# Gate and up products summed in one PSUM bank, with the next outer product's first two products moved between: a decoder layer on one core

## The chip, the cores and the metric

The kernel runs on one core of one Trainium2 chip. The metric is the device time of one execution in microseconds (us). A core has five engines with a queue each: TensorE (PE in the profile, with its weight loads as PEld), VectorE (DVE), ScalarE (ACT), GpSimd (POOL) and SyncE (SP). The program puts matmul results in PSUM banks of 128 x 512 float32, and the other engines copy or add them from there. In this trace an engine's instructions start in the order of its queue, and one that waits holds up those behind it, a DMA's issue included.

## The reference

`x` is [16, 128, 1024] in float32. The reference is one decoder layer:

```python
x = x + attn(layernorm(x))              # one head of 4 of width 1024: 256 wide
x = x + xattn(layernorm(x), ctx_4096)   # linear attention, 8 heads of 64, output normalised
x = x + ffn(layernorm(x))

# ffn:
Wg, Wu, Wd = dequantize(...), dequantize(...), dequantize(...)   # int4, groups of 64
g = jnp.einsum('bsh,ih->bsi', x, Wg)      # h = 1024, i = 2752
u = jnp.einsum('bsh,ih->bsi', x, Wu)
h = jax.nn.silu(g) * u
return jnp.einsum('bsi,hi->bsh', h, Wd)
```

The change touches the products g and u and what turns them into h.

## The kernel before

**Stages.** Self-attention lasts to about 250 us, the second attention to about 806, with its tail beside the first products of the FFN until about 870. The gate and up products follow until 1893, and the down projection until the end. Tokens are in two passes of eight batches; a pass's 1024 tokens are two halves of TB = 512. The 2752 rows of gate and up are eleven blocks: ten of 256 (two halves of 128), and a remainder, RB, of 192. NI = 5 pairs of blocks make the ten.

**Seven products for eight.** All FFN products use the Strassen-Winograd scheme: a 2 x 2 block product takes seven products of sums of blocks. The operands are T1 to T7 on the token side (T1, T2, T3 are blocks themselves; 5, 6, 7 and 4 are differences) and seven weight tiles. The four results are (0,0) = P1+P2, (1,1) = P1+P6+P5+P7, (1,0) = P1+P6+P7+P4 and (0,1) = P1+P6+P5+P3. Some sums are made by accumulating products in one PSUM bank, the rest by DVE.

**Pass 0** (812 to 1388 us, `one_block` and `products`, matmul on line 1069): for each of eleven blocks, a set of seven products of gate and one of up. Each product is eight matmuls (one per K chunk) of 512 columns. The order is `GATE` = 1, 5, 6, 7, 2, 3, 4. A set takes four banks: P1 with P2, P5 with P3, P6 alone, P7 with P4. ScalarE copies P1 (line 1078); DVE adds P6 into `u` (L1081) and P5 into `v` (L1082), then P7 + v, P2's bank as it stands, P3 + u and P4 + u give the results. Gate results go through Silu on ScalarE, up results are multiplied by them into `h`, which is stored to DRAM by `put_stores` (L1019) from ScalarE's queue.

Beside pass 0, the weights of later blocks and of the down projection are made ready by `prepare` (lines 185 to 245): raw int4 is loaded, taken apart and scaled by DVE (`pa`, lines 215 to 217), combined into the seven tiles (`pc`, line 231), and stored to DRAM from ScalarE's queue. One step is taken after those products with `n % 7 in (0, 2, 4, 5)`, and after each product of block 0 once the attention is over (`beside`). Near the end of pass 0, `outer_operand` (L1048) makes pass 1's T5, T6, T7 and T4 on DVE.

**Pass 1, two levels** (1388 to 1845, `two_levels`): for the ten whole blocks the seven outer products of a pair of blocks (order `DOWN` = 1, 2, 6, 5, 3, 7, 4) are each split again into seven inner products of eight matmuls of 256 columns. 35 outer products (5 pairs i by 7 q) of seven inner products (order `INNER2` = 6, 1, 5, 7, 2, 3, 4) run one after the other. GpSimd makes an outer product's left operands (`li`) from weight tiles, DVE the right ones (`ti`; kept from i = 0 for q = 1, 6, 3, 4). ScalarE copies inner P6 (`iu`), DVE adds P1 to it, then P5 for `iv`, and then sums the results into U, V and C over the outer products. After q = 2, 3, 7 and 4 a quadrant C is finished: Silu on ScalarE, `h` on DVE. For the down projection's own seven products `combine_h` makes sums `hc` of h of this pass and h of pass 0, loaded back as `hl`; of each pair of blocks DVE makes one block's and GpSimd the other's. `hc` too are stored by `put_stores` from ScalarE's queue.

**Order.** Instructions through `InOrder` (line 52) stay in the order of the program: in `two_levels` that is TensorE, DVE and GpSimd. Elsewhere the tile scheduler may move instructions of an engine. Small DVE operations of `two_levels` that are not a product's drain wait in a queue `extra`, of which `do_extra` takes one or two after each product. Weight tiles come by SP's queue, in pairs, `AHEAD` = 4 pairs before they are used. The remainder block of pass 1 follows (1845 to 1893), and then the down projection (L1541).

Of the kernel before, what the change touches and what calls it, by code (L numbers as in the profile page):

```python
# [11 lines left out]
F32 = mybir.dt.float32  # L12
# [26 lines left out]
GATE = (1, 5, 6, 7, 2, 3, 4)  # L39
# [16 lines left out]
def decoder_layer(  # L56
# [45 lines left out]
    xt3 = ctx.enter_context(tc.tile_pool(name="xt3", bufs=2, side="right", reuse_waits="tile"))  # L102
# [486 lines left out]
    if True:  # L589
# [156 lines left out]
        def turned(b):  # L746

            xns = []
            for n in range(2):
                xn = xt3.tile([P, C // 2], F32, name="xn3")  # L750

                rows = X[b].rearrange("p (g j e n) -> p n j g e", g=16, j=JC, n=2)[:, n]
                dst = xn.rearrange("p (j g e) -> p j g e", j=JC, g=16)
                normalise_act(dst, rows, b)
                xns.append(xn)
            nc.gpsimd.dma_start(x_all[b], X[b])
            later(2, lambda: turn_rows(b, xns, btr, b2))
            if b == B - 1:
                blocks.update(new_blocks(xlate, lambda k: f"X{HB + 2 * k}"))
                loads = block_loads(0, blocks)  # L760
                for n in range(8):
                    later(7 + 2 * n, lambda: next(loads))
# [170 lines left out]
    with ExitStack() as gs:  # L933
# [29 lines left out]
        HALF = [("g", 1), ("g", 2), ("u", 1), ("u", 2)]  # L963

        def sequence(ps, blk):
            todo = [(mat, q) for mat in "gu" for q in GATE]
            if ps == blk == 0:

                todo = HALF + [k for k in todo if k not in HALF]
            return todo  # L970

        def tiles_of(ps, blk):
            todo = [(blk, *k) for k in sequence(ps, blk)]
# [4 lines left out]
            [t for blk in range(len(BLOCKS)) for t in tiles_of(0, blk)]  # L978
            + [[(2 * i + f, mat, q) for mat in "gu"] for i, q in OUTERS for f in range(2)]
            + tiles_of(1, RB)  # L980
# [34 lines left out]
        def put_stores(now=False):  # L1015
            for st in stores:
                st[0] -= 1
            while stores and (now or stores[0][0] < 0):
                nc.scalar.dma_start(*stores.popleft()[1:])  # L1019
# [29 lines left out]

        def products(blk, mat, T, got):  # L1050
# [4 lines left out]
            def temp(name):  # L1055
                bufs = 2 if name == "p1" else 1
                t = kept[name] = ct.tile([P, TB], F32, name=name, tag=name, bufs=bufs)[:w]
                return t

            def product(q):  # L1060
                wt = next_weights(w)
                put_stores()
                first = {2: 1, 3: 5, 4: 7}.get(q, q)
# [4 lines left out]
                for j in range(JC):  # L1068
# [5 lines left out]
                        stop=(q in (2, 6, 3, 4) and j == JC - 1),  # L1074
                        skip_group_check=True,
                    )
                if q == 1:
                    nc.scalar.copy(temp("p1"), ps)
                elif q == 6:
                    u2 = temp("u2")  # L1080
                    nc.vector.tensor_tensor(u2, ps, kept["p1"], ALU.add)  # L1081
                    nc.vector.tensor_tensor(temp("v"), bank[5], u2, ALU.add)  # L1082
                elif q == 7:
                    got((1, 1), ps, kept["v"])
                elif q == 2:
                    got((0, 0), ps, None)
                elif q == 3:
                    got((0, 1), ps, kept["u2"])
                elif q == 4:
                    got((1, 0), ps, kept["u2"])  # L1090
# [3 lines left out]
        def one_block(ps, blk, T, between):  # L1094
# [38 lines left out]
            for n, (mat, q) in enumerate(sequence(ps, blk)):  # L1133
# [10 lines left out]
        INNER2 = (6, 1, 5, 7, 2, 3, 4)  # L1144
        KEPT = {1: "X8", 6: "X10", 3: "X12", 4: "X14"}
# [4 lines left out]
        def inner_right(T, q, vector=nc.vector):  # L1150
# [9 lines left out]
            def comb(k):  # L1160
                if k == 5:
                    pool, tag = (xlate, KEPT[q]) if q in KEPT else (deep_pool[0], "ti")
# [12 lines left out]
        def inner_left(L):  # L1175
# [9 lines left out]
            def comb(k):  # L1185
                t = L[k] = ct.tile([P, 2, CHUNKS, P], F32, name="li", tag="sg")
                a, b, op = {
                    5: (A(1, 0), A(1, 1), ALU.add),
                    6: (L.get(5), A(0, 0), ALU.subtract),
                    7: (A(0, 0), A(1, 0), ALU.subtract),  # L1190
# [4 lines left out]
            return {k: lambda k=k: comb(k) for k in (5, 6, 7, 3)}  # L1195
# [4 lines left out]
        def two_levels(T, ready):  # L1200
            tensor, vector, gpsimd = (
                InOrder(tc, e) for e in (nc.tensor, nc.vector, nc.gpsimd)
# [7 lines left out]
            extra = deque()  # L1210

            def do_extra(n=None):
                for _ in range(len(extra) if n is None else min(n, len(extra))):
                    extra.popleft()()

            L = ready
            U = V = C = None
            hs = {}
            for n, (i, q) in enumerate(OUTERS):
                banks.rotate(1)  # L1220
                if q == DOWN[0]:
                    U = deep_pool[0].tile(wide, F32, name="U")
                elif q == 5:
                    V = deep_pool[0].tile(wide, F32, name="V")
                load_weights()
                following = {}
                left = inner_left(following) if n + 1 < len(OUTERS) else {}
                if n + 1 < len(OUTERS):

                    extra.extend(inner_right(T, OUTERS[n + 1][1], vector))  # L1230
                if q == 3:
                    halves = {1: load_first(i, 1)}
                bank = {}
                u = v = None

                def got(ib, src, add):
                    k = 2 * ib[0] + ib[1]
                    add_to = vector.tensor_tensor
                    if q == 1:
                        if add is None:  # L1240
                            nc.scalar.copy(U[:, k], src)
                        else:
                            add_to(U[:, k], src, add, ALU.add)
                        return
                    dst, base = {2: (C, U), 6: (U, U), 5: (V, U), 3: (C, V), 7: (C, V), 4: (C, U)}[q]
                    if add is None:
                        if q == 7:
                            add_to(U[:, k], src, U[:, k], ALU.add)
                        add_to(dst[:, k], src, base[:, k], ALU.add)
                        return  # L1250
                    m = V if q == 5 else C
                    add_to(m[:, k], src, add, ALU.add)
                    if q == 7:
                        add_to(U[:, k], U[:, k], m[:, k], ALU.add)
                    add_to(dst[:, k], m[:, k], base[:, k], ALU.add)

                for p in INNER2:
                    set_ = {2: 1, 3: 5, 4: 7}.get(p, p)
                    if set_ == p:
                        bank[p] = banks[0].tile([P, 2, HT], F32, name=f"q{p}", tag="gu")  # L1260
                    ps = bank[set_]
                    for m in range(2):
                        for c in range(CHUNKS):
                            tensor.matmul(
                                ps[:, m, :],
                                L[p][:, m, c, :],
                                R[q, p][:, c, :],

                                start=(set_ == p and m == c == 0),
                                stop=(p in (6, 2, 3, 4) and c == CHUNKS - 1),  # L1270
                                skip_group_check=True,
                            )
                    put_stores()
                    if p == 6:
                        u = ct.tile([P, 2, HT], F32, name="iu", tag="p1", bufs=2)
                        nc.scalar.copy(u, ps)
                    elif p == 1:
                        vector.tensor_tensor(u, ps, u, ALU.add)
                    elif p == 5:
                        v = ct.tile([P, 2, HT], F32, name="iv", tag="v", bufs=1)  # L1280
                        vector.tensor_tensor(v, bank[5], u, ALU.add)
                        for k in (5, 6):
                            if k in left:
                                left[k]()
                    elif p == 7:
                        if q not in (1, 5):

                            C = deep_pool[0].tile(wide, F32, name="C")
                        got((1, 1), ps, v)
                        if left:  # L1290
                            left[7]()
                    elif p == 2:
                        got((0, 0), ps, None)
                    elif p == 3:
                        got((0, 1), ps, u)
                        if left:
                            left[3]()
                    elif p == 4:
                        got((1, 0), ps, u)
                    do_extra({6: 0, 1: 1, 7: 1}.get(p, 2))  # L1300
                load_weights()
                if q in (2, 3, 7, 4):
                    s, half = {2: (0, 0), 3: (0, 1), 7: (1, 1), 4: (1, 0)}[q]
                    nc.scalar.activation(C[:, :, 0], C[:, :, 0], AF.Silu)
                    finish = []
# [348 lines left out]
```

## Time and profile before

| | us |
|---|---|
| runs of before | 2366.76, 2368.12, 2372.04; median 2368.12 |
| profiled execution | 2371.64 |
| its span | 2369.9 |
| TensorE busy in it | 2304.6 |

By stage, from the same profiled execution (busy us of an engine in the stretch):

| stretch, us | stage | PE | DVE | ACT | POOL |
|---|---|---|---|---|---|
| 0-250 | self-attention | 239.4 | 167.6 | 36.7 | 56.5 |
| 250-812 | second attention | 549.0 | 471.1 | 326.4 | 138.7 |
| 812-1388 | pass 0 of gate and up | 563.0 | 349.0 | 69.1 | 9.0 |
| 1388-1845 | pass 1, two levels | 433.0 | 377.2 | 42.0 | 247.1 |
| 1845-1893 | pass 1, remainder block | 48.0 | 18.5 | 4.5 | 5.8 |
| 1893-2370 | down projection | 472.2 | 242.2 | 8.1 | 0.0 |

The profiled execution is one, and its times are read against its own 2371.64. Names in the profile are the program's tiles: `q` is a PSUM bank of an inner product, `p` one of pass 0's, `w` a weight tile, `wg<-pa` a store of prepared gate weights. L52 stands for all that goes through `InOrder`, so there the tile names tell what an instruction is. "[2.54 <-DVE iu L52]" behind an instruction says that its engine was idle for 2.54 us before it and that the DVE operation writing `iu` ended the wait.

### The profile page before, as it was taken

How to read it: one execution, taken by the hardware profiler on the slowest of the kernel's cores; microseconds unless marked ns; L12 is line 12 of the kernel's file. 1: busy time of each engine (PE TensorE's matmuls, PEld its weight loads, DVE VectorE, ACT ScalarE, POOL GpSimd, SP SyncE). 2: the span in 40 equal slices, each digit the busy share in tenths (PEclk: the TensorE clock that was granted, in tenths of full speed). 3: DMA queues.
4: the chain of work that ended last, by engine and by line, in shares of the span. 5: the costliest groups of instructions: out<-in, count | busy, mean ns of one | idle time of the engine just before them, and what ended most of it. 6: DMA issues, size and time to landing. Idle time of an engine off the chain costs nothing.

```text
span 2369.9 us, 25410 instructions
## 1 busy us (share of the span) xinstructions
PE 2304.6 (97%) x8976; PEld 1589.8 (67%) x8976; DVE 1625.4 (69%) x2318; ACT 486.8 (21%) x771; POOL 457.0 (19%) x321
## 2 busy tenths in 40 slices
PE   8999999999999899999899999999999999999999
PEld 7556566666666554444344468778778488888888
DVE  6694788888879639997641179788887474444562
ACT  2111356566656440000000000000010000000000
POOL 4120122222222200000000035564564100000000
PEclk9999999999999999999999999999999999999999
DMA  6232366566685549999953224553553864544631
GB/s 237 74 121 86 121 168 185 179 178 183 191 242 170 169 141 344 357 365 351 305 185 102 74 93 131 172 186 107 178 203 101 295 214 144 166 143 144 214 111 36
DMA packets 275774, 424.69 MB, mean 179 GB/s; under 512 B 26752, under 2 KB 124928, under 8 KB 275520
## 3 DMA queue, kind: packets, MB, share of 16 engines
q1 hardware_dynamic: 207824, 310.52, 42.5%
q10 hardware_dynamic: 65520, 104.16, 12.2%
q0 software_dynamic: 2304, 8.39, 0.9%
q8 instruction: 72, 1.18, 0.2%
q14 instruction: 54, 0.44, 0.1%
HBM read 265.62 MB, written 157.35 MB: 178 GB/s over the span
## 4 chain that ended last, share of the span: by engine, by line
PE 76%; DVE 13%; DMA 7%; issue 2%; ACT 1%; SPq 0%; POOL 0%; ACTq 0%; DVEq 0%; POOLq 0%
PE po L1541 20%; PE p L1069 14%; PE q L52 12%; PE mm L52 11%; PE kq L52 8%; PE mm L368 5%; PE tr L52 3%; DVE hc L52 2%; PE mm L383 2%; DVE C L52 2%; PE mm L264 2%; DVE pa L216 1%; DVE pa L217 1%; DVE pc L231 1%; DMA wg<-pa 1%
## 5 line engine op out<-in xcount | busy, mean ns | idle before, releaser
L1069 PE MATMUL p<-b,w 128*128 128x512 f32 (+1 forms) x768 | 344.2, 599 | 16.2 <-DVE v L1082 6.2
L1069 PEld LDWEIGHTS p<-b,w 128*128 128x128 f32 (+1 forms) x768 | 143.1, 188 | 204.1 <-issue 185.8
L1069 PE MATMUL p<-T,w 128*128 128x512 f32 (+1 forms) x576 | 255.1, 592 | 0.0
L52 POOL TENSOR_TENSOR li<-w 128x512 f32<-128x512 f32 x70 | 97.5, 1393 | 564.1 <-DVE h L1113 501.7
L1069 PEld LDWEIGHTS p<-T,w 128*128 128x128 f32 (+1 forms) x576 | 106.8, 185 | 140.0 <-issue 136.2
L52 PE MATMUL q<-ti,li 128*128 128x256 f32 x840 | 192.8, 379 | 0.6 <-DVE ti L52 0.6
L1541 PE MATMUL po<-wc,lc 128*128 128x256 f32 x840 | 183.4, 379 | 0.0
L52 PEld LDWEIGHTS q<-ti,li 128*128 128x128 f32 x840 | 159.5, 190 | 23.1 <-POOL li L52 1.0
L1541 PEld LDWEIGHTS po<-wc,lc 128*128 128x128 f32 x840 | 159.6, 190 | 21.8
L684 POOL TENSOR_TENSOR qe<-qe,qden 128x1024 f32<-128x1024 f32 x64 | 121.7, 1901 | 266.1 <-DVE qden L52 231.7
L1541 PE MATMUL po<-wq,lq 128*128 128x256 f32 x560 | 126.7, 379 | 0.4 <-issue 0.4
L52 PE MATMUL mm<-kh,cxt 128*128 128x256 f32 x512 | 123.5, 384 | 3.4 <-DMA kh<-kd 3.2
L52 PE MATMUL kq<-cx,wk_sb 128*128 128x512 f32 x256 | 121.6, 597 | 3.5 <-ACT ke L641 3.5
L52 PEld LDWEIGHTS mm<-qs,m_sb 128*128 128x128 f32 x512 | 97.3, 190 | 39.1 <-issue 28.7
L52 PE MATMUL kq<-wq_sb,xn 128*128 128x512 f32 x256 | 120.4, 593 | 0.0
L52 PE MATMUL mm<-qs,m_sb 128*128 128x256 f32 x512 | 120.3, 379 | 0.0
L52 DVE TENSOR_REDUCE qmx<-kq 128x16 f32<-128x1024 f32 x64 | 76.3, 1193 | 62.9 <-PE kq L52 62.8
L52 PEld LDWEIGHTS mm<-kh,cxt 128*128 128x128 f32 x512 | 96.4, 191 | 33.5 <-issue 18.3
L1541 PEld LDWEIGHTS po<-wq,lq 128*128 128x128 f32 x560 | 106.0, 190 | 16.0 <-issue 1.0
L368 PE MATMUL mm<-xnT,wqkv_sb 128*128 128x512 f32 (+1 forms) x320 | 112.5, 508 | 0.0
L52 PE MATMUL q<-b,w 128*128 128x256 f32 x320 | 81.2, 399 | 21.2 <-DVE iu L52 21.2
L368 PEld LDWEIGHTS mm<-xnT,wqkv_sb 128*128 128x128 f32 x320 | 59.8, 190 | 45.0 <-issue 41.6
(206 smaller groups left out, 3765.3 us busy)
## 6 DMA issues: line engine op xcount, KB each, us to landing
w<-wg SPq DMA_DIRECT2D x140, 256.0 KB, 2.9
w<-wu SPq DMA_DIRECT2D x140, 256.0 KB, 3.4
lq<-h SPq DMA_DIRECT2D x140, 256.0 KB, 4.3
kd<-kt SPq DMA_DIRECT2D x64, 512.0 KB, 3.5
kh<-kd SPq DMA_DIRECT2D x128, 256.0 KB, 5.6
h<-hc ACTq DMA_DIRECT2D x80, 256.0 KB, 2.8
wq<-wd SPq DMA_DIRECT2D x70, 256.0 KB, 5.0
h<-h ACTq DMA_DIRECT2D x60, 256.0 KB, 3.7
```

What stands on the lines that cost most here:

```text
L52: return lambda *args, **kw: self._tc.keep_in_program_order(fn(*args, **kw))
L216: vector.tensor_tensor(shaped(a), nib, zero, ALU.subtract)
L217: vector.tensor_tensor(shaped(a), shaped(a), scale, ALU.mult)
L231: vector.tensor_tensor(t, a, b, op)
L264: tensor.matmul(ps, oT[:, d, ts(b % BPT, S)], wo_d[d][:, ts(h, 512)], start=(d == 0), stop=(d == 1),)
L368: nc.tensor.matmul(ps[:, tokens], wqkv_sb[:, f, c, :], xnT[:, c, tokens], start=(c == 0), stop=(c == CC - 1),)
L383: nc.tensor.matmul(ps, xnT[:, c, ts(i, S)], wqkv_sb[:, 4:6, c, :], start=(c == 0), stop=(c == CC - 1),)
L684: nc.gpsimd.tensor_tensor(qe, qe, den.unsqueeze(2).to_broadcast(wide), ALU.mult)
L1069: nc.tensor.matmul(ps, wt[:, j, :], T[q][:, j, :], start=(first == q and j == 0), stop=(q in (2, 6, 3, 4) and j == JC - 1), skip_group_che ...
L1541: nc.tensor.matmul(bank[:, i, :], l[:, ts(i, S)], w,  start=(start and c == 0 and i % 2 == 0), stop=(stop and c == len(pairs) - 1), skip_g ...
```

## The change

**Sums in one bank.** `GATE` becomes 1, 7, 6, 2, 5, 4, 3. In one bank P1, then P6, P5 and P3 are accumulated; P4 goes into P7's bank; P2 has its own. A set takes three banks. ScalarE copies the bank after P1 (`k1`), P7 (`k7`) and P6 (`k6`, which then holds P1+P6). DVE makes (0,0) from P2's bank and k1, (1,1) from the bank after P5 and k7, (1,0) from P7's bank after P4 and k6; (0,1) is the bank after P3 as it stands. `u` and `v` are gone. The same holds for the inner products of `two_levels`.

**Order on TensorE in `two_levels`.** In outer product n: 6, 2, 5, 4 of n, then 1 of n+1, then 3 of n, then 7 of n+1. The first two of all run ahead of the loop. GpSimd makes left operands in the order 7, 5, 6, 3.

**Who does what.** All `hc` are made by DVE. Stores in `two_levels` go out on SP; ScalarE is now in program order there. The old h, `hl`, are loaded for half 1 at the end of q = 3 and for half 0 at the end of the next pair's q = 1 (before: at the end of q = 4). The right operands kept from i = 0 are those of q = 1, 6, 5, 4, 7.

**Preparation.** `or blk == 0` is gone, so block 0 takes a preparation step after the same products as the others. Block 0's own order (`HALF`) is gone. T1's operands 5, 6, 7 are made after up's P5 of the last block of pass 0, 4 after its P4. The tile `xn3` comes from another pool of the same two buffers.

```diff
-GATE = (1, 5, 6, 7, 2, 3, 4)
+GATE = (1, 7, 6, 2, 5, 4, 3)
...
-            while stores and (now or stores[0][0] < 0):
-                nc.scalar.dma_start(*stores.popleft()[1:])
+                queue.dma_start(*stores.popleft()[1:])
...
-                first = {2: 1, 3: 5, 4: 7}.get(q, q)
+                first = {6: 1, 5: 1, 3: 1, 4: 7}.get(q, q)
...
-                if q == 1:
-                    nc.scalar.copy(temp("p1"), ps)
-                elif q == 6:
-                    u2 = temp("u2")
-                    nc.vector.tensor_tensor(u2, ps, kept["p1"], ALU.add)
-                    nc.vector.tensor_tensor(temp("v"), bank[5], u2, ALU.add)
-                elif q == 7:
-                    got((1, 1), ps, kept["v"])
-                elif q == 2:
-                    got((0, 0), ps, None)
+                if q in (1, 7, 6):
+                    keep(q, ps)
                 elif q == 2:
+                    got((0, 0), ps, kept[1])
+                elif q == 5:
+                    got((1, 1), ps, kept[7])
+                elif q == 4:
+                    got((1, 0), ps, kept[6])
                 elif q == 3:
-                    got((0, 1), ps, kept["u2"])
-                elif q == 4:
-                    got((1, 0), ps, kept["u2"])
+                    got((0, 1), ps, None)
...
-        INNER2 = (6, 1, 5, 7, 2, 3, 4)
-        KEPT = {1: "X8", 6: "X10", 3: "X12", 4: "X14"}
+        KEPT = {1: "X8", 6: "X10", 5: "X12", 4: "X14", 7: "t7"}
...
+            def multiply(n, p):
...
+                if p in (1, 7, 6):
+                    t = state[n]["kept"][p] = ct.tile(
+                        [P, 2, HT], F32, name="k", tag=f"k{p}", bufs=2 if p == 1 else 1
+                    )
+                    scalar.copy(t, ps)
+                put_stores(queue=nc.sync)
...
+                    left(7)
+                multiply(n, 6)
+                do_extra(2)
...
+                    soon_due.extend(inner_right(T, OUTERS[n + 1][1], vector))
+                multiply(n, 2)
+                got(n, (0, 0), 2, 1)
+                do_extra(1)
+                multiply(n, 5)
+                got(n, (1, 1), 1, 7)
+                if not last:
+                    left(5)
+                    left(6)
+                do_extra(1)
+                multiply(n, 4)
+                got(n, (1, 0), 7, 6)
+                do_extra(2)
+                if not last:
+                    multiply(n + 1, 1)
+                    do_extra(2)
+                multiply(n, 3)
+                got(n, (0, 1), 1, None)
+                if not last:
+                    left(3)
+                do_extra(1)
+                load_weights()
+                if not last:
+                    do_extra(len(soon_due))
+                    multiply(n + 1, 7)
+                if q in (2, 3, 7, 4):
+                    finish(i, q)
                 if q == 3:
-                    halves = {1: load_first(i, 1)}
+                    while extra:
+                        extra.popleft()()
+                    hl = load_first(i, 1)
+                elif q == 7:
+                    soon_due.append(lambda i=i, hl=hl: combine(i, 1, hl))
+                elif q == 1 and i > 0 or last:
+                    do_extra(len(soon_due) + len(extra))
+                    hl = load_first(i if last else i - 1, 0)
+                    combine(i if last else i - 1, 0, hl)
...
-            elif n % 7 in (0, 2, 4, 5) or blk == 0:
+            elif n % 7 in (0, 2, 4, 5):
                 next(rest, None)
...
-                elif q in (5, 6):
-                    outer_operand(T1, q)
-                    if q == 6:
-                        outer_operand(T1, 7)
+                elif q in (5, 4):
+                    for k in {5: (5, 6, 7), 4: (4,)}[q]:
+                        outer_operand(T1, k)
...
-        outer_operand(T1, 4)
```

## The prediction

> **What bounds the kernel now.** I read the busy table first, then busy time by stage, then the list of TensorE's waits, then single stretches of the timeline on the way of the longest wait.
>
> ```profile
> PE 2304.6 (97%) x8976; PEld 1589.8 (67%) x8976; DVE 1625.4 (69%) x2318; ACT 486.8 (21%) x771; POOL 457.0 (19%) x321
> ...
> 1060.00:1141.00 81.00, 73.82 (x168) 31.97 (x166) 61.16 (x118) 6.74 (x11) 0.00 (x0) 0.98 1.00 344
> 1141.00:1388.00 247.00, 246.99 (x576) 106.44 (x577) 97.90 (x152) 18.26 (x30) 3.80 (x3) 1.00 0.48 151
> 1388.00:1845.00 457.00, 432.99 (x1963) 376.23 (x1962) 377.15 (x458) 41.97 (x59) 247.08 (x173) 0.99 0.45 149
> ```
>
> The stage rows give the stretch and its length, busy PE, PEld, DVE, ACT and POOL, then granted clock, DMA share and GB/s. TensorE is the bound everywhere, and the change removes no matmul. So it can only win TensorE's idle time and half-clock time. In 1388-1845 (the two-level stage) that is 24 us; in 1060-1141 (end of pass 0's weight preparation) it is 7 us; in 1141-1388 nothing. The waits name them (total, times, longest):
>
> ```profile
> PE q L52 <- DVE iu L52: 22.4, 9, 3.1
> ...
> PE p L1069 <- DVE v L1082: 6.2, 5, 2.5
> PE p L1069 <- DMA w<-wg: 6.0, 1, 6.0
> PE p L1069 <- ACT p L1078: 4.0, 1, 4.0
> ```
>
> **Two-level stage, what goes.** A product is 8 matmuls, 1.727 us; an outer product has seven, and an undisturbed one took 12.085 us. 35 x 12.085 = 423.0. The stage ran 1388.3 to 1845.2 = 456.8, so 33.9 us are lost: waits of 22.4 (iu) + 1.0 (iv) + 0.6 (ti) = 24.0, four half-clock stretches (below) 6.8, restarts the other 3. The wait for iu is only nominally DVE's. ScalarE (ACT; ACTq is its DMA issuing), then VectorE, then TensorE:
>
> ```profile
> 1577.14 0.57 ACT L1276 COPY iu<-q 128x512 f32<-128x512 f32 x1
> ...
> 1585.60 6.38 ACTq L1019 DMA_DIRECT2D h<-hc  x8
> 1592.02 0.59 ACT L1276 COPY iu<-q 128x512 f32<-128x512 f32 x1 [10.80 <-DMA h<-hc]
> ```
> ```profile
> 1592.64 0.69 DVE L52 TENSOR_TENSOR iu<-q,iu 128x512 f32<-128x512 f32 x1 [1.50 <-ACT iu L1276]
> ```
> ```profile
> 1593.39 3.47 PE L52 MATMUL q<-b,w 128*128 128x256 f32 x8 [2.54 <-DVE iu L52]
> ```
>
> The copy of product 6 stands on ScalarE's queue behind eight stores of hc. The stores wait for the hc sums, half of which are GpSimd's:
>
> ```profile
> L52 POOL TENSOR_TENSOR hc<-hl,h x10: 1260/1714/1717, 1470.3 to 1855.8; 128x512 f32<-128x512 f32 x10
> L52 DVE TENSOR_TENSOR hc<-hl,h x10: 694/1750/1753, 1475.2 to 1853.8; 128x512 f32<-128x512 f32 x10
> ```
>
> (min/median/max ns.) In after.py the stores leave from SyncE, all hc are DVE's, and ScalarE keeps copies, Silu and table loads. So the 24.0 go. The 65 hc stores now queue on SP among its weight loads; the stage's DMA share is 0.45 and weights are fetched four pairs ahead, so I cost that at nothing. If a store that waits for its hc held SP for the 10.8 us that ACT was held, four pairs (each lasts half an outer product, 6.0 us) still cover it.
>
> The clock, in stretches of 3.4 us (the PEclk column, seventh value from the window's length on):
>
> ```profile
> 1578.50:1581.90 3.40, 3.40 (x16) 3.01 (x17) 3.37 (x6) 0.59 (x1) 0.00 (x0) 1.00 1.01 368
> 1593.70:1597.10 3.40, 3.40 (x10) 2.67 (x9) 2.02 (x4) 0.00 (x0) 1.13 (x1) 0.51 0.00 0
> ```
>
> After the 2.5 us wait before 1593.4 TensorE ran one stretch at 0.51, which costs 1.7 us; after a 2.74 us wait before 1578.5 it ran at 1.00. There are four half-rate stretches, 6.8 us; waits under 2 us had none. I let 1.4 of the 6.8 remain.
>
> The Trainium skill ("TensorE: Matmul & The Clock Gate", section "Part 1: The HAM clock gate") has the clock fall only after a whole idle window of about 3.4 us. By that rule no wait here would have halved it and removing the waits would return nothing of the 6.8; that would leave 8 us of gain where I have 13. The trace has three such stretches after waits of 2.5 us, so the rows decide.
>
> **Two-level stage, what comes.** DVE loses 35 iu, 35 iv and 16 ti, and takes 40 hc: at about 0.68 us the stage's 377 us of DVE become near 310. TensorE's new order is 6, 2, 5, 4, next 1, 3, next 7. Each temporary or sum has at least one product (1.73 us) between its drain and the product that writes over it; a copy takes 0.59 us, a DVE sum 0.68. On an undisturbed outer product that hides all. Where it doesn't:
> - Start: the first product 6 needs left operand 6 from GpSimd, whose buffer is freed by the last gate tiles; these are read by DVE behind the operands T5, T6, T7, T4 (2.28 us each, now all ahead of it). I count 3.1; bounds 0 and the four, 9.1.
> - i=0, outer product 7: eleven sums, four ti and two h are 17 x 0.68 = 11.6 of 12.1 us, and the next product 7 needs the last ti. 2.7; bounds 0 and 4, as before's ti waits were 0.6 and its longest wait here 3.1.
> - Each i from 1: the second halves' old h are loaded late, into the one hl buffer, after the last hc of the other half. Loads land in a median 4.6 us, after issues of 0.43; DVE, in order, stands 5.9 us at its first hc. Eight operations behind it (5.4) come before product 3 of outer product 2 may overwrite. Products 6, 2, 5, 4, 1 cover 8.6 and the start of the load about 1: wait 1.7. And product 5 of the following outer product waits for the copy k6, which follows a Silu (1.06) that waits on DVE: 1.2. 2.9 x 4 = 11.6; bounds 0 (DVE caught up) and 4 x 4.6 = 18.
>
> Sum 17.4, range 8 to 26. Lost time goes from 33.9 to 17.4 + 1.4 + some 2 of restarts = 20.8: **13 us won**, range 4 to 24.
>
> **Pass 0.** Per set DVE loses u and v (0.68 each), ScalarE gains two copies (0.59). But cover shrinks. Before, a drain by DVE had two products (6.9 us at 3.44) until the bank or temporary was written over, the copy of product 1 three (10.3). After, the copies k1 and k6 and the sum (1,1) each have one, 3.44. During preparation (895-1140) DVE is busy 98% and DMA share near 1, and DVE falls behind:
>
> ```profile
> 1119.40 0.76 DVE L215 TENSOR_SCALAR pa<-raw 128x512 int32<-128x512 int32 x2 [12.57 <-DMA raw<-in_dq]
> ...
> 1133.43 5.13 PE L1069 MATMUL p<-b,w 128*128 128x512 f32 x8 [4.00 <-ACT p L1078]
> ```
>
> There one preparation step waited 12.6 us for its raw weights, the drains queued behind it, and TensorE lost 4.0 + 6.2 + a half-rate stretch. From the trace, u started 3.3 to 7.1 us behind its product in blocks 2 to 5, 13.1 at worst (the copy, 13.7). A lag is a backlog: TensorE waits once and it is worked off, so a cover shorter by 3.44 costs about that once per episode. One or two episodes are 3.4 to 7: I take +5. Below: -3, as DVE's work per block is less and preparation ends a block earlier. Above: 20 to 25 (rival). "Even preparation" drops block 0's steps at every product; the total stays and work per block 1 to 4 is about 196 us of DVE against 192.6 of TensorE, as before.
>
> The first block's 6.0 wait for w<-wg stays. Two more table loads (1.28 each) fall beside TensorE work. Block 10, down projection and all ahead of 812 have the same work: 0.
>
> **Sum.** 2371.64 (profiled execution; span 2369.9) - 13 + 5 = 2363.6. That execution is 3.5 above the median of the runs, 2368.12, so the forecast is **2360**, its own range 2350 to 2366.
>
> **Rivals.**
> - Full gain (2343). All 24.0 and the 6.8 come back, and only the start (3.1) and i=0 (2.7) cost: -25, pass 0 free. For it: ScalarE has little left and DVE drops by 67 us. Against: the late hl load sits at the head of an in-order DVE.
> - Slower (2379): one mechanism, cover of one product in pass 0 while preparation runs. If the lag comes anew in each set because preparation steps stand ahead of the drain, eight sets of blocks 2 to 5 wait (5.2 mean lag - 3.44) = 1.8, 14 us; four half-rate stretches add 6.8, the worst lag another 3.4: +24 - 13 = +11. It decides once the added waits in 862-1141 pass 13 us. For it: DVE 98% busy. Against: backlog is worked off while TensorE waits.
> - A wash (2368): hl loads at the upper bound (18), start 5, i=0 3: new waits 26, gain 5, pass 0 +5. This is also the case in which moved stores change little.
>
> **How the numbers follow.** Forecast 0.48, full gain 0.12, slower 0.28, wash 0.12. About 0.2% (4.7 us) can be told from no change. Faster: 0.12 + 0.43 of the forecast's 0.48 = 0.55. Same: the wash and the forecast's upper edge, 0.17. Slower 0.28. The range runs from just under the full gain to just above the slower case, 2342 to 2381, leaving out the tails of both.
>
> **What would show it.** Right: no wait for iu, no hc store on ACTq, ScalarE's copies within 1 us of their product; the stage from first to last outer product at about 444 us; waits at outer product 2, product 3, for DVE, about 1.7 each; block waits of some 15 us in 862-1141. Wrong: waits of TensorE for ACT k in pass 0 in most sets (the slower rival); waits for left operands (GpSimd) in every outer product, which I cost at nothing since one takes 1.39 us and four fit in 12.1; weight waits (w<-wg) in the stage, which would make SP's stores the cost.

## The result and the profile after

After takes 2382.07 us (median of 4 runs, 2378.11 to 2384.94), before 2368.82 in the same comparison: a ratio of 1.0054, 95% interval 1.0034 to 1.0073. The change makes the kernel slower by 0.5%. The profiled execution of after is 2383.05, its span 2381.3.

The stages, from the first matmul of each to the next in the two profiled executions:

| stage | before, us | after, us | difference |
|---|---|---|---|
| up to the first gate product | 812.8 | 814.4 | +1.6 (code unchanged but for xn3's pool; the runs below have 810.4 to 815.4) |
| pass 0 | 575.5 | 587.4 | +11.9 |
| two levels | 456.7 | 454.6 | -2.1 |
| remainder block | 48.1 | 48.1 | 0 |
| down projection | 476.8 | 476.8 | 0 |

So two terms went wrong: pass 0, where I had +5, and the two-level stage, where I had -13. After's busy times by stage, in the columns of the prediction's stage rows (stretch, length, PE, PEld, DVE, ACT, POOL, granted clock, DMA share, GB/s):

```profile
862.00:1060.00 198.00, 187.98 (x445) 82.37 (x444) 173.02 (x318) 31.12 (x48) 1.51 (x2) 0.99 0.97 335
1060.00:1141.00 81.00, 70.14 (x158) 29.89 (x157) 57.76 (x112) 9.66 (x16) 0.00 (x0) 0.98 0.98 338
1402.00:1856.00 454.00, 435.34 (x1959) 378.43 (x1958) 322.55 (x408) 82.51 (x129) 193.11 (x139) 0.97 0.45 150
```

In 862-1141 TensorE is idle 20.9 us (before 11.2: 4.0 and 7.2). In the two-level stage DVE fell from 377 to 323, and yet TensorE is idle 18.7 us, at a mean clock of 0.97 (before 0.99). After's waits of TensorE (total, times, longest):

```profile
PE p L1063 <- ACT k L1052: 16.8, 10, 3.8
PE q L52 <- ACT k L52: 11.1, 6, 2.9
...
PE p L1063 <- DMA w<-wg: 6.1, 1, 6.1
PE q L52 <- DVE ti L52: 4.3, 2, 3.4
...
PE q L52 <- POOL li L52: 3.3, 1, 3.3
...
PE p L1063 <- DVE sg L1094: 2.1, 3, 1.0
PE p L1063 <- DVE h L1102: 1.4, 2, 0.9
```

The waits for iu, v and p are gone; two waits for ScalarE's new copies k stand in their place, one in each stage. In pass 0 TensorE waited 20.3 us (16.8 + 2.1 + 1.4) for k and drains, against 10.2 before.

**Pass 0.** ScalarE in one of these stretches of after (its DMA issues as ACTq), then TensorE:

```profile
904.92 2.30 ACTq L187 DMA_DIRECT2D wu<-pc  x3
908.38 0.33 ACTq L187 DMA_DIRECT2D wg<-pa  x1
908.80 0.59 ACT L1052 COPY k<-p 128x512 f32<-128x512 f32 x1 [4.11 <-DMA wu<-pc]
```
```profile
909.44 2.80 PE L1063 MATMUL p<-T,w 128*128 128x512 f32 x3 [2.41 <-ACT k L1052]
```

The copy k stands behind four stores of prepared weights, and TensorE starts again 0.05 us after it ends. That looks like the two-level stage of before: a copy in a queue of stores. It was my first theory, and by itself it does not explain the loss, as the runs below show.

Half of the 20.3 us, 10.5, fell into block 4 alone (1050 to 1112 us). There DVE was busy for 76% of the time, against 89 to 96% in blocks 1 to 3. It stood 14.9 us for DMA instead, 6.6 of them for raw weights. TensorE, then DVE:

```profile
1099.84 2.91 PE L1063 MATMUL p<-T,w 128*128 128x512 f32 x4 [3.82 <-ACT k L1052]
```
```profile
1101.42 0.63 DVE L214 TENSOR_SCALAR pa<-raw 128x384 int32<-128x384 int32 x2 [5.23 <-DMA raw<-in_uq]
```

**Two levels.** After at outer product 9, counted from 0 (q = 6 of the second pair), DVE, ScalarE and TensorE:

```profile
1527.52 1.75 DVE L52 TENSOR_TENSOR hc<-h 128x512 f32<-128x512 f32 x1
1529.31 1.64 DVE L52 TENSOR_TENSOR hc<-hc,hl 128x512 f32<-128x512 f32 x1
1530.99 1.64 DVE L52 TENSOR_TENSOR hc<-hl,hc 128x512 f32<-128x512 f32 x1
1532.55 0.68 DVE L52 TENSOR_TENSOR C<-q,U 128x512 f32<-128x512 f32 x1
```
```profile
1533.26 1.06 ACT L52 ACTIVATE C<-C 128x1024 f32<-128x1024 f32 x1 [4.11 <-DVE C L52]
1534.23 0.57 ACT L52 COPY k<-q 128x512 f32<-128x512 f32 x1
```
```profile
1534.84 3.78 PE L52 MATMUL q<-ti,li 128*128 128x256 f32 x8 [2.86 <-ACT k L52]
```

The last sum C of a quadrant is behind a run of hc; the Silu waits for C; the copy k6 waits behind the Silu; product 5 waits for k6. The eight matmuls then took 3.78 us instead of 1.89, at half clock.

### The profile page after: what moved, and what is told of

The parts are those of the page before. It is cut to its first block, busy times and chain, and to the rows that moved or that the text cites. A ratio compares the mean times of both kernels' runs of the same rounds, so it can differ in the third digit from the quotient of the medians.

```text
span 2381.3 us, 25380 instructions
## 1 busy us (share of the span) xinstructions
PE 2312.3 (97%) x8976; PEld 1592.2 (67%) x8976; DVE 1544.7 (65%) x2224; ACT 558.1 (23%) x891; POOL 398.0 (17%) x281
## 4 chain that ended last, share of the span: by engine, by line
PE 78%; DVE 12%; DMA 6%; issue 3%; ACT 1%; POOL 1%; SPq 0%; DVEq 0%; ACTq 0%; POOLq 0%
PE po L1550 20%; PE p L1063 15%; PE q L52 13%; PE mm L52 11%; PE kq L52 8%; PE mm L367 5%; PE tr L52 3%; DVE hc L52 2%; PE mm L382 2%; DVE pa L215 2%; PE mm L263 2%; DVE pa L216 1%; DMA wu<-pa 1%; DMA wg<-pa 1%; DVE pc L230 1%
## 5 line engine op out<-in xcount | busy, mean ns | idle before, releaser
L1063 PE MATMUL p<-T,w 128*128 128x512 f32 (+1 forms) x576 | 260.1, 601 | 16.8 <-ACT k L1052 16.8
L52 PE MATMUL q<-ti,li 128*128 128x256 f32 x840 | 201.8, 391 | 18.7 <-ACT k L52 11.1
L52 ACT COPY k<-q 128x512 f32<-128x512 f32 x105 | 61.3, 584 | 350.1 <-PE q L52 350.1
L1052 ACT COPY k<-p 128x512 f32<-128x512 f32 (+1 forms) x72 | 42.1, 585 | 351.3 <-PE p L1063 134.9
```

Source lines behind the costliest of these rows:

```text
L52: return lambda *args, **kw: self._tc.keep_in_program_order(fn(*args, **kw))
L1052: nc.scalar.copy(t, ps)
L1063: nc.tensor.matmul(ps, wt[:, j, :], T[q][:, j, :], start=(first == q and j == 0), stop=(q in (2, 3, 4) and j == JC - 1), skip_group_check= ...
```

## The experiments

Times are medians in us; each ratio is to the runs of before made beside it, whose median moved between 2368.8 and 2373.2, so compare rows by their ratios. Pass 0 and the stage are from the run's one profiled execution.

| run | kernel | time | ratio, 95% | pass 0 | two levels |
|---|---|---|---|---|---|
| (after) | | 2382.07 | 1.0054 [1.0034, 1.0073] | 587.4 | 454.6 |
| e1_stores_pool | after, prepared stores on GpSimd | 2379.61 | 1.0034 [1.0019, 1.0049] | 588.7 | 452.6 |
| e1_stores_sync | after, prepared stores on SyncE | 2349.91 | 0.9909 [0.9889, 0.9930] | 561.7 | 448.5 |
| e2_silu_late | after, Silu behind k6 | 2372.41 | 1.0001 [0.9990, 1.0012] | 588.2 | 447.1 |
| e3_old_pass0 | after, products of pass 0 as before | 2361.70 | 0.9958 [0.9941, 0.9975] | 578.0 | 444.5 |
| e4_before_prep_sync | before, prepared stores on SyncE | 2359.62 | 0.9942 [0.9921, 0.9963] | 562.1 | 459.5 |
| e5_before_h_sync | before, h and hc stores on SyncE | 2366.94 | 0.9971 [0.9959, 0.9984] | 573.7 | 452.5 |
| e6_t_late | e1_stores_sync, T7 and T4 later | 2358.13 | 0.9933 [0.9914, 0.9952] | 562.1 | 457.1 |
| e7_all_edits | four edits | 2345.31 | 0.9880 [0.9862, 0.9898] | 560.9 | 443.5 |
| e8_t_spread | e7, T6, T7, T4 spread | 2338.12 | 0.9861 [0.9843, 0.9879] | 562.3 | 438.0 |
| e9_hc_later | hc one outer product later | 2349.32 | 0.9909 [0.9894, 0.9924] | 562.3 | 446.7 |
| e10_best | e8 and e9 | 2340.80 | 0.9877 [0.9863, 0.9892] | 561.0 | 440.2 |
| e11_before_both | e4 and e5 | 2355.31 | 0.9933 [0.9915, 0.9950] | 561.7 | 452.7 |
| e12_paced | after, preparation in program order | 2355.59 | 0.9934 [0.9912, 0.9955] | 559.7 | 453.7 |
| e13_paced_pool | e12, prepared stores on GpSimd | 2356.85 | 0.9935 [0.9915, 0.9956] | 559.8 | 460.0 |
| e14_before_paced | before, preparation in program order | 2358.19 | 0.9939 [0.9921, 0.9956] | 561.4 | 456.1 |
| e15_paced_best | e12 with the repairs of e8 | 2334.85 | 0.9844 [0.9825, 0.9862] | 559.9 | 438.3 |

### Pass 0: the queue or the crowd

**e1_stores_pool and e1_stores_sync** move the stores of prepared weights off ScalarE:

```diff
-            rest = prepare(jobs, 2, nc.scalar)
+            rest = prepare(jobs, 2, nc.gpsimd)     # e1_stores_pool
+            rest = prepare(jobs, 2, nc.sync)       # e1_stores_sync
```

> After, with one edit: the stores of prepared weights beside pass 0 leave from GpSimd's queue and no more from ScalarE's. Theory A (ScalarE's copies k stand behind stores that wait for DVE's preparation): the 16.8 us of waits for k in pass 0 fall to under 4, pass 0 comes from 587.4 to about 572 to 576 us, the whole from 2382 to about 2368. Rival (DVE itself is behind, the store queue only shows it): waits turn from ACT k to DVE sums, pass 0 stays within 3 us of 587, the whole at about 2381.

> As the run before, but the stores of prepared weights leave from SyncE's queue, among the loads of raw weights and of weight tiles. Theory A: waits for k go here as well. But a store that waits for DVE now holds up the loads behind it, so I expect waits for w or raw: pass 0 between 575 and 600 us, the whole 2370 to 2395. Rival (DVE is behind): as after, 2381.

The two disagree. On GpSimd the whole is 2.5 us shorter, which the intervals do not tell from nothing, and pass 0 is no shorter; the waits turn to DVE's drains, as the rival said:

```profile
PE p L1063 <- DVE h L1102: 13.4, 3, 8.8
PE p L1063 <- DVE sg L1094: 8.7, 4, 2.5
```

On SyncE all 20 us went, and pass 0 and the whole came below both expectations. Either ScalarE's queue is not the cause by itself, or the two runs differ in something else. The same stretch of e1_stores_sync shows what else had changed (to be read against 862-1060 above):

```profile
862.00:1060.00 198.00, 197.32 (x479) 88.83 (x477) 155.06 (x277) 34.10 (x54) 1.51 (x2) 1.00 0.88 293
```

DVE is busy 155 us instead of 173, DMA share is 0.88 instead of 0.97. Counted in the traces, preparation in blocks 1 to 4 has 71, 73, 75, 77 DVE operations in before, 79, 80, 79, 81 in after, but 77, 59, 47, 51 in e1_stores_sync, where it lasts to block 9 (to 1319 us; after: to 1208). With the stores among SyncE's loads the scheduler places the preparation later. That gave a new theory (F): pass 0 is slow because the preparation is pressed into blocks 1 to 6, and the store queue only decides which wait shows it.

**e12_paced, e13_paced_pool, e14_before_paced** spread the preparation without the queue (e12), with it (e13), and in before (e14):

```diff
-            rest = prepare(jobs, 2, nc.scalar)
+            rest = prepare(jobs, 2, nc.scalar, InOrder(tc, nc.vector))   # e12, e14; nc.gpsimd in e13
```

> After, with one edit: the DVE operations of the preparation beside pass 0 keep their place in the program, so that the scheduler no longer moves them forward (about 45 to 60 per block's sets instead of 85 to 110); their stores stay on ScalarE's queue. Theory F (pass 0 is slow because preparation is pressed into blocks 1 to 6, and stores on SyncE helped only since they spread it): pass 0 from 587.4 to 562 to 566, the whole from 2382 to 2357 to 2360. Theory A (the stores on ScalarE's queue are the cause): waits for k stay, pass 0 at 575 or more, the whole above 2370.

> As e12_paced, with the stores of prepared weights on GpSimd's queue as well. Theory F: as e12_paced, within 3 us (2357 to 2360). Theory A, or both causes at once: 2357 to 2360 here, but e12_paced is at least 5 us longer.

> Before, with the same one edit (preparation in the order of the program, stores on ScalarE). Theory F: pass 0 from 575.5 to 562 to 564, the two-level stage at 457 to 460, the whole from 2371 to about 2359; so before and after have the same pass 0 once it is spread, and the one bank costs something only beside pressed preparation. Theory A: the waits for v and p stay and pass 0 is over 570.

Theory F holds in all three: pass 0 is 559.7, 559.8 and 561.4, with 42 or 43 preparation operations in each of blocks 1 to 9 (51 in e14's block 1). In e12 the stores are still on ScalarE, and of TensorE's waits in pass 0 only that for the first weights is left:

```profile
PE p L1063 <- DMA w<-wg: 6.0, 1, 6.0
```
```profile
862.00:1060.00 198.00, 197.92 (x480) 89.37 (x479) 122.83 (x206) 34.28 (x53) 1.14 (x2) 1.00 0.75 244
```

DVE is at 123 of 198 us, DMA at 0.75. So the spread alone is enough, and once the preparation is spread, to free ScalarE's queue is worth nothing (e12 and e13 alike). Whether DVE or DMA is the crowded one these runs do not tell, since spreading eases both. The spread has a price at the start of the two-level stage: the wait for li there is 5.1 us in e12 and 7.9 in e13, against 3.3 in after.

What a free queue is worth beside pressed preparation stays open. In e1_stores_pool it won nothing, but GpSimd's stores also landed later there (5.5 to 6.7 us against 4.4 to 5.2), and so did the raw weights. Against that stands block 1 of e1_stores_sync: 77 operations, DVE 98% busy, and no wait of TensorE, where after, with 79 operations and the stores on ScalarE, waited 3.3 us in block 1.

**e3_old_pass0** takes back the products of pass 0 (order, banks, u and v on DVE, T1's operands); the code of the preparation is after's:

> After, with pass 0 and the remainder block as in before (order of products, four banks, u and v by DVE, T1's operands where they were); the two-level stage is after's, the preparation too (block 0 takes no extra steps). Theory A: pass 0 is back at about 575.5 us, the two-level stage stays at 452 to 455, the whole at about 2369. Rival (the even preparation made pass 0 longer, not the copies): pass 0 stays at 583 or more, the whole at 2378.

Pass 0 is 578.0, so 9.4 of the 11.9 us (587.4 - 578.0) went. But the preparation did not stay as it was in after: it has 71, 77, 73 and 80 operations in blocks 1 to 4, 301 in all, against 319 in after and 296 in before. So the 9.4 us are the shorter cover and the heavier crowd together, and no run here parts them; the other 2.5 belong to what stayed. The stage of 444.5, ten below after's, was not expected: no wait for li at its start (3.3), 2.4 us less for k, and 3.6 us less half-clock time (see the clock below).

**e4_before_prep_sync** is the edit of e1_stores_sync in before:

> Before, with one edit: the stores of prepared weights leave from SyncE's queue instead of ScalarE's. Theory A (these stores hold ScalarE up in both kernels, and the cover only sets how much of it TensorE sees): before's 10.2 us of waits of pass 0 (v, and the copy p) go too, pass 0 comes from 575.5 to about 563, the two-level stage stays at 457, the whole at about 2360. Rival (only one bank for all sums makes pass 0 quick once the queue is free): pass 0 stays over 570, the whole above 2366.

562.1, as in e1_stores_sync. With the preparation spread, before's four banks a set and after's three make no difference to pass 0 (e14 561.4, e12 559.7).

### Two levels: copy, Silu, operands

**e2_silu_late** is after with the Silu one copy later:

```diff
                 multiply(n, 6)
+                if pending:
+                    finish(*pending.pop())
                 do_extra(2)
...
                 if q in (2, 3, 7, 4):
-                    finish(i, q)
+                    pending.append((i, q))
+                    if last:
+                        finish(*pending.pop())
...
                 elif q == 7:
+                    finish(*pending.pop())
```

> After, with one edit in the two-level stage: the Silu of a finished quadrant (but the one of outer product 7) is put on ScalarE's queue behind the copy of the next outer product's P6, no more ahead of it. Theory B (k6 stands behind a Silu that waits for DVE; each such wait of 2.86 us also costs two half-clock stretches, 3.3 us): the 11.1 us of waits for k go, with them some 10 us of clock; the stage comes from 454.8 to about 435, the whole from 2382 to about 2363. Rival (DVE is late by the hc sums, and TensorE waits for DVE's drains instead): waits of about 2 us for C or U at the same places, the stage at 450 to 455, the whole 2378 to 2382.

In between: the waits for k in the stage went (11.1 to none), but 6.1 us of waits for DVE's C came, most of 1.4 each, and the ti wait rose from 4.3 to 5.8; the stage won 7.5, not 20. The copy did stand behind the Silu, and behind that DVE is late.

**e5_before_h_sync** and **e11_before_both**, in before:

```diff
-        def put_stores(now=False):
+        def put_stores(now=False, queue=nc.scalar):
...
-                    put_stores()                       # in two_levels
+                    put_stores(queue=nc.sync)
```

> Before, with one edit: in the two-level stage the stores of h and hc leave from SyncE's queue instead of ScalarE's; order, banks and GpSimd's half of hc stay. Theory C (the 22.4 us of waits for iu came from those stores alone): the waits for iu and their half-clock time go, the stage comes from 457 to about 428 to 432, the whole from 2371 to about 2343. Rival (the next outer product's P1 and P7 in between are what is needed, since GpSimd's hc and DVE's sums are late themselves): the stage stays above 445, the whole above 2358.

> Before with both queues freed: stores of prepared weights beside pass 0 and stores of h and hc in the two-level stage leave from SyncE; order, banks, GpSimd's hc as in before. It tells what of the change's own order is worth anything: from the single edits, pass 0 562 and the stage 452.5, the whole about 2354, against 2350 for after with its one queue freed. Rival (the order of after is needed for the two-level stage): this one above 2358.

Theory C fell: 17.4 of the 22.4 us of waits for iu remain, in both. Of the two longer waits of a pair, one fell from 2.7 to 0.6 us and the other grew from 2.5 to 3.4. DVE, then TensorE, in e5_before_h_sync:

```profile
1587.71 1.64 DVE L52 TENSOR_TENSOR hc<-hc,hl 128x512 f32<-128x512 f32 x1
1589.38 1.63 DVE L52 TENSOR_TENSOR hc<-hl,hc 128x512 f32<-128x512 f32 x1
1590.93 0.68 DVE L52 TENSOR_TENSOR iu<-q,iu 128x512 f32<-128x512 f32 x1
```
```profile
1591.67 3.46 PE L52 MATMUL q<-b,w 128*128 128x256 f32 x8 [3.40 <-DVE iu L52]
```

The copy was done long before (1583.1); the sum iu stands behind hc of 1.64 us in DVE's own queue. Before's stores on ScalarE hid this second holder. The stage won 4 us, where 25 to 29 were expected. e11 came as the sum of the single edits, 2355.31 for 2354.

**e6_t_late** and **e8_t_spread** look for the 3.3 us at the start:

```diff
-                    for k in {5: (5, 6, 7), 4: (4,)}[q]:
+                    for k in {5: (5,), 4: (6,)}[q]:                  # e6
+        outer_operand(T1, 7); outer_operand(T1, 4)                   # e6, ahead of two_levels
...
+                if n < 3:                                            # e8, in two_levels; T5 stays
+                    soon_due.append(lambda n=n: outer_operand(T, (6, 7, 4)[n], vector))
```

> After with stores of prepared weights on SyncE, and one more edit: of pass 1's operands T5, T6, T7, T4, DVE makes T7 and T4 (2.28 us each) behind the last sums of pass 0 instead of ahead of them. If those stand ahead of the h that free GpSimd's buffer, the wait for li at the start (3.3 us and its half-clock time of 1.9) goes: the stage from 448.5 to about 444, the whole from 2350 to 2346. Rival (the left operands are late for GpSimd's own time): the 3.3 us stay, the whole at 2350.

> After with stores of prepared weights on SyncE, the late Silu and P7's right operand first, and T6, T7 and T4 made one by one in the first three outer products instead of in one piece behind pass 0 (T5 stays there). Theory D (at the start GpSimd's sum for the left operand takes 7 to 8 us instead of 1.26 because DVE's 2.28 us sums run beside it, not because a buffer is held): li at the start takes under 2 us, the wait of 3.3 to 3.9 us and its 1.5 us of half clock go, the stage from 443.5 to about 439, the whole from 2345 to 2340. Rival (the buffer of sg is held by the h sums): the wait stays over 2 us, the whole 2344 to 2346.

In e6 the wait stayed, at 3.9. GpSimd in after, with the TensorE product that waited for its third sum (the left operand of product 6):

```profile
1398.85 8.19 POOL L52 TENSOR_TENSOR li<-w 128x512 f32<-128x512 f32 x1 [4.25 <-DVE h L1103]
1407.12 1.59 POOL L52 TENSOR_TENSOR li<-li,w 128x512 f32<-128x512 f32 x1
```
```profile
1408.77 3.78 PE L52 MATMUL q<-ti,li 128*128 128x256 f32 x8 [3.31 <-POOL li L52]
```

GpSimd in e8, the sum that took 8.19 us in after:

```profile
1374.58 1.26 POOL L52 TENSOR_TENSOR li<-w 128x512 f32<-128x512 f32 x1 [4.25 <-DVE h L1103]
```

Both stood 4.25 us for the buffer; it is the operation itself that takes 8.19 us beside DVE's three sums of 2.28 and 1.26 without them. In e8 the wait is gone and the stage is 438.0, as theory D said. The Trainium skill ("SBUF — State Buffer", section "SBUF: two separate sides") gives a reason: a DVE instruction with two SBUF inputs and a GpSimd instruction that reads SBUF lock one shared pair of ports, and the one that starts first has it for the whole instruction. The 8.19 agrees with a sum that stood until all three of DVE's were over (3 x 2.28 + 1.26 = 8.10), which is longer than one instruction.

The buffer had a share too. By the semaphores in after's trace the third sum took over the buffer that TensorE's product 7 read until 1405.5, and in e12_paced the third sum stood 2.94 us for that buffer before it took 4.93. So in after some 1.6 us of the 3.3 (1407.1 - 1405.5, an estimate), 1.9 with the third sum's own 0.3, are the slow sum's. In e8 the third sum got a buffer that DVE freed, so that run took away both.

e6's stage is also 8.6 us longer than e1_stores_sync's, though its waits are longer by 0.6 us only; it has 7.8 us more of half-clock time (see the clock below).

**e7_all_edits** joins e1_stores_sync, e2_silu_late, e6_t_late, and P7's right operand first, since P7 now is multiplied second:

```diff
-            return [lambda k=k: comb(k) for k in (5, 6, 7, 4)]
+            return [lambda k=k: comb(k) for k in (7, 5, 6, 4)]
```

> After with four edits: stores of prepared weights on SyncE, Silu behind the copy of the next P6, T7 and T4 behind the last sums of pass 0, and in the two-level stage the right operand for P7 made first of the four (P7 is now multiplied second). If the remaining waits are those named (k 11.8, li 3.3, ti 4.2, each with half-clock time), pass 0 is 562, the stage about 430 and the whole about 2331. If DVE only becomes late elsewhere (6 us of waits for C showed with the late Silu): stage 438 to 445, the whole 2340 to 2346.

The stage is 443.5, within the second expectation: the ti wait went from 4.2 to 3.3, li has the 3.9 of e6, and C has 6.1.

**e9_hc_later** puts the hc of half 0 one outer product on; **e10_best** joins it with e8:

```diff
                     hl = load_first(i if last else i - 1, 0)
-                    combine(i if last else i - 1, 0, hl)
+                    if last:
+                        combine(i, 0, hl)
+                elif q == 2 and i > 0:
+                    combine(i - 1, 0, hl)
```

> After with stores of prepared weights on SyncE, the late Silu and P7's right operand first, T6, T7 and T4 where after has them; the hc of half 0 are put into DVE's queue one outer product later (behind q = 2 instead of q = 1, their loads still issued at the end of q = 1). Theory E (the last stalls of 1.39 us for C come from DVE standing 3.8 us at its first hc for the load, with eight hc behind it in the outer product that also finishes a quadrant): the waits for C (6.1 us) go, the stage from 443.5 to about 438, the whole about 2339. Rival (DVE is merely full there): the wait moves one outer product on and keeps over 4 us, the whole 2343 to 2346.

> The two edits of the runs t_spread and hc_later together, with stores of prepared weights on SyncE, the late Silu and P7's right operand first. If both theories D and E hold: the stage at 431 to 434, the whole at about 2334, the fastest of all. If only one holds: 2338 to 2341.

Theory E fell: the waits for C became waits for V, 5.5 us (4 of 1.4), one outer product on, and k came back with 2.6. That is what the rival (DVE is merely full there) expected. e10 is no faster than e8.

**e15_paced_best** is e8 with the preparation in program order and its stores on ScalarE:

> After with preparation in the order of the program (stores on ScalarE), the late Silu, P7's right operand first, and T6, T7 and T4 one by one in the first three outer products: the run t_spread with the order of the program in place of stores on SyncE. Theory F: pass 0 562 to 565, the stage 436 to 440, the whole 2337 to 2342. Theory A: 2350 or more.

2334.85, 1.6% below before (0.9844, 0.9825 to 0.9862); its interval overlaps that of e8 (0.9843 to 0.9879). What it still waits for in the FFN is 6.2 us for the first weights, 6.4 for C and 3.3 for ti.

### The clock

Three waits of the same length, 2.85 us, at the same place of three pairs in after. The two stretches of 3.4 us that follow each (clock in the seventh value):

```profile
1534.80:1538.20 3.40, 3.36 (x8) 2.74 (x9) 2.22 (x4) 0.00 (x0) 0.00 (x0) 0.50 0.34 127
1538.20:1541.60 3.40, 3.40 (x10) 2.73 (x10) 1.82 (x2) 0.00 (x0) 1.27 (x1) 0.58 0.00 0
1626.70:1630.10 3.40, 3.36 (x9) 2.71 (x10) 2.22 (x4) 0.00 (x0) 0.00 (x0) 0.54 0.37 139
1630.10:1633.50 3.40, 3.40 (x17) 3.01 (x16) 3.08 (x4) 0.00 (x0) 1.27 (x1) 1.00 0.13 17
1717.10:1720.50 3.40, 3.40 (x16) 3.01 (x17) 3.23 (x6) 0.00 (x0) 1.27 (x1) 1.00 0.33 116
1720.50:1723.90 3.40, 3.40 (x18) 2.99 (x17) 1.87 (x3) 0.59 (x1) 0.04 (x1) 1.00 0.55 156
```

Half clock lasts 6, 3 and 0 us after one and the same wait. The starts of matmuls, 0.216 us apart at full clock, are 0.43 apart there; summed, that cost 3.0, 1.5 and 0. After's stage lost 10.2 us so (with 2.9 each after the waits for li, 3.3, and ti, 3.4), before's 7.2, and e1_stores_sync's 3.6, with almost the same waits as after: so its stage is 6 us shorter. The length of the wait alone does not decide it. What does, no run here tried; that a wait meets a period of the clock's own at different points would fit, but is not shown.

## Why the prediction was wrong, step by step

- **Sign and size.** I forecast 2360 and gave the slower rival 0.28 at 2379; 2382 is a microsecond outside the range. The profiled execution is 19.5 us above its forecast of 2363.6: pass 0 is 6.9 of it (11.9 for +5), the two-level stage 10.9 (-2.1 for -13), and 1.6 arose ahead of the FFN. Of the 10.9, half-clock time is 8.8 (10.2 for 1.4), waits are 1.3 (18.7 for 17.4), restarts the rest.
- **The step that failed most: "I let 1.4 of the 6.8 remain."** New waits were forecast at 17.4 and measured at 18.7 (11.1 + 4.3 + 3.3): near in sum, and near by item (11.6, 2.7, 3.1), though in other places than forecast, which was luck. But half-clock time rose to 10.2. Of it, 5.8 came after the waits for li and ti, which I had forecast at 3.1 and 2.7 myself; before's own trace has half clock after four of its eight waits of 2.3 to 3.1 us, and the sum gave these two none. The other 4.5 came because I had split the wait of a pair into 1.7 and 1.2, both in the region where before showed none, and it came as one of 2.86. A count of waits was not enough; each length had to be checked against the clock rows. The rule cited there, by which only an idle window of about 3.4 us lowers the clock, would have covered at most the 2.9 us after the ti wait of 3.43; the waits of 2.86 and 3.31 are shorter. And in e1_stores_sync the same ti wait of 3.43 was followed by full clock.
- **"The wait for iu is only nominally DVE's"** was wrong for 17.4 of 22.4 us (e5, e11). Two queues held the same product, and the trace names one. The waits for iu still went, with the new order, but DVE's runs of hc stayed and came back as the waits for k6, through C and Silu (and for C itself in e2).
- **Place of the new waits.** Product 3 after the hl load did not wait at all (forecast 1.7): DVE did stand 4.0 us there and caught up. Product 5 of q = 6 waited 2.86, not 1.2, in three pairs, and three other copies k cost 0.84 each; the last pair had no 2.86.
- **Start.** 3.1 forecast, 3.3 measured: near by luck. I had put it all on a buffer freed late by DVE; some 1.9 us (the estimate above) are GpSimd's slow sum beside DVE, and the buffer was TensorE's product 7 to free.
- **Pass 0, "a lag is a backlog: TensorE waits once and it is worked off".** It waited 15 times in blocks 1 to 5, 10 of them for k, 20.3 us in all: while preparation is pressed, the lag is new in each block. This is near the slower rival's mechanism, at 12 us instead of 24. But I read the crowd wrongly. "DVE is busy 98%" over 895 to 1140 us is not what before's trace has: it is 89% there (218.8 of 245 us), and in 1100 to 1120, where the 12.57 us wait for raw weights lies, 32%. So DMA, with its share near 1, is as much the crowded one as DVE, and after's largest block of waits (block 4) looks the same.
- **"Even preparation ... the total stays"** took the program's order for the engine's. The scheduler moves these operations forward by blocks in either kernel; kept in order (e12, e14) they cost pass 0 nothing. So before's own 10 us of waits in pass 0 were to be had by one edit (e4, e14), and the number of banks does not matter then.
- **What was right**: stores off ScalarE at no cost on SyncE, no weight wait in the stage (w<-wg only at 814), DVE's load in the stage (310 forecast, 323 measured), the remainder block and the down projection unchanged.

What stays open: why the last pair has no 2.86 us wait, what decides how long half clock lasts after a wait, and, in pass 0, how much of the 11.9 us is the shorter cover and how much the heavier crowd.

## What to carry to other kernels

When a copy waits behind stores, ask what the stores wait for, before moving them: here they waited for DVE's pressed preparation, and moving them to GpSimd's queue won pass 0 nothing, while spreading the work won 27 us of it. See where the scheduler really put background work (count its operations per block in the trace), and pin it if it runs ahead. In a chain through several in-order engines, take the holder named by the trace as the last of several, and price a remaining wait with its half-clock time: in these runs waits of up to 1.5 us were followed by no half-clock stretch, and waits of 2.85 us by up to 3.0 us of loss.

## What the runs showed of the hardware

- GpSimd's 128x512 sum took 1.26 us alone and 8.19 beside three DVE sums of 2.28 us on SBUF (after). Of DVE's hc in after, 28 of the 39 that ran beside a GpSimd sum took over 1 us, up to 1.76; the other 49 took 0.68 to 0.69.
- A TensorE wait of 2.85 us was followed by half clock for 6, 3 or 0 us (after).
- Stores of 256 KB issued by GpSimd landed in 5.5 to 6.7 us (median by kind), those by ScalarE in 4.4 to 5.2 (after); loads took longer beside them too, raw weights 5.8 to 6.9 instead of 5.0 to 5.6. GpSimd was busy 75 us of 862-1060 (before and after: 1.5).
